# ScalarE sums for two group norms, a fifth weight tile, and the first pre-sum ahead of GpSimd's multiply

## The chip, the cores and the metric

The kernel runs on one core of a Trainium2 chip. A core has five engines that run side by side, each with its own queue of instructions in a fixed order: TensorE (PE, matmuls), VectorE (DVE), ScalarE (ACT), GpSimd (POOL) and SyncE (SP, which here only issues DMAs). They wait for one another by semaphores. The metric is device time in microseconds (us), here a median of three runs; one further execution was profiled.

## The reference

Two layers of "outlook attention" on an image batch x of shape (8, 56, 56, 384), float32. In each layer x is normalised by groups (32 groups of 12 channels, mean and variance over a whole image), and the layer's result is added to x:

```python
def _gn(v, G=32, eps=1e-5):
    g = v.reshape(B_, H_, W_, G, C_ // G)
    m = jnp.mean(g, axis=(1, 2, 4), keepdims=True)
    s = jnp.var(g, axis=(1, 2, 4), keepdims=True)
    return ((g - m) / jnp.sqrt(s + eps)).reshape(v.shape)
x = x + _L0_conv_ref(_gn(x), Wv, Wa, Wo)
x = x + _L1_conv_ref(_gn(x), W_attn, b_attn, W_v, b_v, W_proj, b_proj)
```

Layer 0 has 12 heads. For each pixel it projects x to values v and to 9 x 9 logits a head, takes a softmax over the last 9, weighs the 3 x 3 neighbourhood of v with each of the 9 rows, folds the 9 results back onto the 3 x 3 neighbourhood (a sum of overlapping patches), and projects with Wo. Layer 1 has 6 heads and one row of 9 weights a pixel.

What matters here: before a pixel of a layer can be normalised, the sums over its whole image must be known.

## The kernel before, in words

**Tiling.** The 8 images are worked on in 4 pairs (IMG = 2). A column x of both images, 112 rows, is the unit of layer 0: W = 56 columns a pair, 224 columns in all, one loop step each. Channels lie on the 128 partitions in 3 chunks (NCH). Columns go in groups of SB = 8: the 8 x 112 rows of a group fill 7 tiles of 128 (column j of the group, j = 0 to 6, brings 112 of its own rows and 16 rows of column 7). So a step with j = 7 (NTILE) has no projections of its own; its weights are gathered by DMAs in `share_out` (L664).

**A step of layer 0** (L942 to L985, `attend` L621). For each pi of 0 to 2 TensorE projects a third of the logits into a PSUM bank (288 columns, `project`), VectorE takes the maximum and subtracts it into the tile `at`, and `between(pi)` puts other work in that place of all queues. Then ScalarE takes exp of `at`, TensorE projects v, ScalarE copies v out, and `between(3)` follows. PE, DVE, ACT and POOL keep the order in which the program issues; nothing is reordered by a scheduler.

What `between` adds (L959 to L979), with the column that it works for:

- `normalise` (L694), for the column before: VectorE sums the exps (four adds, a reciprocal, a mask: "den"), GpSimd multiplies `at` with den (972 elements, the longest GpSimd operation).
- `presum` (L707), for two columns before: fold needs sums over neighbouring columns. GpSimd makes them in three operations into the tile `pre`; the first adds two terms of columns c and c - 1, the others need column c + 1, which is normalised in this step. In `between(3)` ScalarE copies two more terms into `pre`.
- `fold` (L741), for three columns before: ScalarE and VectorE write the weights `wts`; TensorE shifts rows with a 0/1 matrix into `pw` (four matmuls); two to four DMAs by SP bring the weights to a table in DRAM.
- `jobs` (L354, L809 `plan`): for each patch of PX = 7 columns, matmuls that contract values with weights (`pc`, read out to `yT` by ScalarE), and six `project_out` jobs (L851): three matmuls into `po`, VectorE adds the residual into `x1t`, and in the version before takes the batch statistics of layer 1's input (`bn_stats`, two images). Steps at which jobs are due are written out by hand in `plan`.
- `stats_chunk` (L461), for the next pair: VectorE transposes a third of a block of 4 columns of x (`xt`), takes the batch statistics of both images, and every third step SP stores the block in DRAM (`keep_block` L486). It runs in steps with c from 3 to 44 of pairs 0 to 2. Pair 0's own statistics are taken ahead of the loop, as there is no other work then.

`norm_params` (L272) turns the statistics into scale and bias: VectorE aggregates them, TensorE sums over the channels of a group with a matmul (`pgmean`, then `pgvar`), ScalarE takes a square root. It is in three parts, put into steps c = 45 to 47 (x, from `upkeep` L896) and, for layer 1's input, into the last job's step and the two after it (`norms`, L885 to L891).

**Buffers that the change touches.** `at` has 4 buffers (L630, L681): column c's is read until `presum(c + 1)` is through in step c + 3, so that step c + 4 takes the buffer in which c was. `pre` has 2, `x1t` 2, `xt` 2, PSUM 4 banks for projections, one each for `po`, `pw`.

**Layer 1** (L1022 onward) is a loop over the same columns with its own steps; the change adds a call there that does work in its first steps alone.

Of the kernel before, what the change touches and what calls it, by code (L numbers as in the profile page):

```python
# [15 lines left out]
def two_outlook_layers(  # L16
# [35 lines left out]
    P = 128  # L52
# [214 lines left out]
    def sort_columns(t, by, i, engine):  # L267
        engine(
            t[:, i].rearrange("k (j p) -> k j p", j=NCH), by[:, i].rearrange("k (p j) -> k j p", j=NCH)
        )  # L270

    def norm_params(st, name, params, key):  # L272

        mv = stat.tile([P, IMG, 2], F32, tag="mv", name=f"mv_{name}")

        def over_groups(src, what):
            pg = ps.tile([P, IMG], F32, tag="o", name=f"p{what}_{name}")
            matmul(pg, gmat, src, start=True, stop=True)
            g = stat.tile([P, IMG], F32, tag=what, name=f"{what}_{name}")
            vector.tensor_copy(g, pg)  # L280
            return g

        for b in range(IMG):
            vector.bn_aggr(mv[:, b, :], st[:, b].rearrange("p i n s -> p (i n) s"))
        yield
        mean = over_groups(mv[:, :, 0], "gmean")

        part = stat.tile([P, IMG], F32, tag="part", name=f"part_{name}")
        vector.tensor_sub(part, mv[:, :, 0], mean)
        vector.tensor_mul(part, part, part)  # L290
        vector.tensor_add(part, part, mv[:, :, 1])
        yield
        var = over_groups(part, "gvar")
        std = stat.tile([P, IMG], F32, tag="std", name=f"std_{name}")
        scalar.activation(std, var, AF.Sqrt, bias=eps_t)
        scale = const.tile([P, IMG], F32, name=f"scale_{name}")
# [86 lines left out]
    gpsimd.memset(zs[1][:, NZ0:], 0.0)  # L383
    zs = [z[:, :NZ0].rearrange("p (n e) -> p n e", n=NPY0) for z in zs]
    jobs, norms = Jobs(), Jobs()
    later = []

    def flush():
        while later:
# [32 lines left out]
    def layer0(late, pools):  # L422
# [38 lines left out]
        def stats_chunk(pair, blk, i):  # L461

            if blk == 0 and i == 0:
                stats[pair] = stat.tile([P, IMG, NCH, NBLK, 6], F32, tag="st0", name=f"st0_{pair}")
            if i == 0 and pair:
                xts[pair, blk] = block_tile(pair, blk)
            xr, xt = xrs[pair, blk], xts[pair, blk]
            if pair == 0:
                pt = bank(P, 0, XB * R).rearrange("p (m r) -> p m r", m=XB)
                for j in range(XB):  # L470
                    transpose(pt[:, j, :], xr[:, j, i::NCH], ident[:R, :R])
                scalar.copy(xt[:, :, i, :], pt)
            else:
                vector.transpose(
                    xt[:, :, i, :].rearrange("p m (k s) -> p s m k", s=NR), xr[:, :, :, i::NCH]
                )
            yield
            for b in range(IMG):
                vector.bn_stats(stats[pair][:, b, i, blk, :], xt[:, :, i, b * H : (b + 1) * H])
            if i == NCH - 1:  # L480
                del xrs[pair, blk]
                if pair:
                    keep_block(pair, blk)
            yield

        def keep_block(pair, blk):  # L486

# [133 lines left out]
        def attend(pair, c, between):  # L621

            nm = f"0_{pair}_{c}"
            k, j = divmod(c, SB)
            if j == NTILE:
                for n in range(K + 1):
                    between(n)
                return
            lhs = xns[(pair * W // SB + k) % 2][:, :, j, :]
            at = work.tile([P, K, K2, PH], F32, tag="at", name=f"at_{nm}", bufs=4)  # L630
            mx = work.tile([P, K, PH], F32, tag="mx", name=f"mx_{nm}", bufs=1)
            for pi in range(K):
# [31 lines left out]
        def share_out(pair, c):  # L664

            k, j = divmod(c, SB)
            at, last = attns[pair, c], lasts[(pair * W // SB + k) % 2]
            end = c - j + NTILE
            if j < NTILE - 2:
                later.append(  # L670
                    lambda: sync.dma_start(
                        bass.AP(
                            last.tensor, last.offset + j * PART * NA0,
                            [[H * NA0, IMG], [NA0, PART], [1, NA0]],
                        ),
                        at[R:].rearrange("p a b c -> p (a b c)"),
                    )
                )
                return
            if j == NTILE - 2:  # L680
                attns[pair, end] = work.tile([P, K, K2, PH], F32, tag="at", name=f"at_0_{pair}_{end}", bufs=4)  # L681
# [25 lines left out]
        def presum(pair, c):  # L707
# [17 lines left out]
                    gpsimd.tensor_tensor(dst, terms[0], terms[1], ALU.add)  # L725

            put(1, 2, of(0, 1, 2), of(-1, 1, 2))
            put(3, 1, of(0, 3, 1), of(1, 3, 1))
            put(2, 1, pre[:, :, 2:3, :], of(1, 2, 1)) if c + 1 < W else None
            pres[pair, c] = pre  # L730
# [78 lines left out]
        def plan(pair, px, first, second, last):  # L809
# [36 lines left out]
            if pair == NPAIR - 1 and px == NPX - 1:  # L846
                jobs.add(second[-1], clear_bands)
            if px == 0:
                st1s[pair] = stat.tile([P, IMG, NCH, 2 * NPX, 6], F32, tag="st1", name=f"st1_{pair}")

            def project_out(half, j):  # L851
                lo, hi = HALVES[half]
# [10 lines left out]
                for b in range(IMG):  # L863
                    vector.bn_stats(
                        st1s[pair][:, b, j, 2 * px + half, :],
                        x1t[:, j, : hi - lo, b * H : (b + 1) * H],
                    )
                if j == NCH - 1:
                    later.append(
                        lambda: sync.dma_start(  # L870
# [13 lines left out]
            if px == NPX - 1:  # L884
                def params_part(n):  # L885
                    if n == 0:
                        making["1"] = norm_params(st1s.pop(pair), f"1_{pair}", params1, pair)
                    next(making["1"])

                for n in range(3):  # L890
                    norms.add(last[-1] + n, lambda n=n: params_part(n))  # L891

        making = {}
        clearing = list(clears())
# [44 lines left out]
        for step in range(NPAIR * W + LAG):  # L939
# [4 lines left out]
            def weigh():  # L944

                normal = 1 <= step < NPAIR * W + 1 and (step - 1) % SB < NTILE
                if normal:
                    normalise(*divmod(step - 1, W))
                if normal and step % SB == NTILE:
                    share_out(*divmod(step - 1, W))  # L950
                if 2 <= step < NPAIR * W + 2:
                    summing.append(presum(*divmod(step - 2, W)))
                    next(summing[0])
                if normal and step % SB < NTILE:
                    share_out(*divmod(step - 1, W))
                if normal:
                    keep_v(*divmod(step - 1, W))

            def between(n):  # L959

                if n == 0:
                    next(turning, None)
                    weigh()
                    jobs.run(step, 1)
                elif n == 1:
                    if step % SB != NTILE:
                        next(folding, None)
                    next(turning, None)
                elif n == 2:
                    jobs.run(step, 1)  # L970
                    norms.run(step, 1)
                else:
                    for part in summing:
# [48 lines left out]
    def layer1(pools, base, last_of_layer0, late_w):  # L1022
# [226 lines left out]
        for step in range((NG + 1) * PX):  # L1249
# [23 lines left out]
            if g and m == moved:  # L1273
                move(done)
            jobs.run(base + step, 1)
            norms.run(base + step, 1)
            flush()
            store()
# [57 lines left out]
```

## Time and profile before

| what | value |
|---|---|
| median of 3 runs | 3263.03 us (3261.41 to 3264.24) |
| profiled execution | 3258.23 us |
| its span (first to last instruction) | 3256.5 us |
| granted TensorE clock, mean | 0.977 |
| VectorE batch statistics in the layer 0 loop | 636, of 0.33 to 0.39 us |
| ScalarE normalise, 128x672 / 128x504 | 0.95 / 0.81 us |
| ScalarE exp, 128x972 | 1.01 us, 196 of them |
| GpSimd multiply, 128x972 | 2.25 us |
| activation table loads | 17, of 1.28 us |

The profile's page has each engine's busy time; groups of instructions (line, engine, operation, output<-inputs, shapes, count, then busy time and mean ns of one); and waits (an engine's idle time in front of a group, by what ended it). Most instructions of the loop are issued through one helper and carry its line, L143 (L128 for matmuls), so groups are told apart by tile names. The windows view gives busy time by stretch of the span, with the granted clock (PEclk, 1.00 is full speed) and the DMA engines' share. Layer 0's loop runs from about 70 us to 2149 us.

### The profile page before, as it was taken

The page shows a single profiled execution, that of the slowest core. Times are in us where ns is not written, and L with a number is a line of the kernel's source. Part 1 is how long each engine was busy: PE and PEld are TensorE (multiplying, and loading weights), DVE is VectorE, ACT ScalarE, POOL GpSimd, SP SyncE. Part 2 cuts the span into 40 slices and gives each one's busy share as a digit, 9 for nine tenths or more (in the row PEclk, how much of TensorE's full clock was granted, in tenths as well). Part 3 has the DMA queues.
Part 4 walks back from the last instruction along what each step waited for, and adds up shares of the span by engine and source line. Part 5 has one row for each costly group of instructions (what it writes and reads, how often), then busy time and mean ns, then how long its engine had stood idle before and what let it go on. Part 6 is the DMA issues. An engine that isn't in the chain of part 4 may idle for free. (4 is left out here: it accounts for less than half of the span.)

```text
span 3256.5 us, 71940 instructions
## 1 busy us (share of the span) xinstructions
PE 3049.7 (94%) x27136; PEld 2044.7 (63%) x27136; DVE 2182.2 (67%) x5071; ACT 1020.7 (31%) x2736; POOL 1531.4 (47%) x2319
## 2 busy tenths in 40 slices
PE   6789999989999999999999999979999999999998
PEld 5556666666666766666666667745565656565655
DVE  5778777788887688887767677734555555555554
ACT  3233334333333433333334333322222222222221
POOL 2555445455445555454555555544434334343331
PEclk8999999999999999999999999989999999999999
DMA  9699997899998889998778788797888989989887
GB/s 285 193 280 307 294 283 244 275 297 285 280 281 292 271 265 288 302 305 269 259 252 297 258 286 284 228 336 211 224 237 229 247 222 243 237 235 232 242 227 170
DMA packets 745405, 850.80 MB, mean 261 GB/s; under 512 B 406286, under 2 KB 632210, under 8 KB 736738
## 3 DMA queue, kind: packets, MB, share of 16 engines
q1 hardware_dynamic: 647890, 711.32, 73.4%
q0 software_dynamic: 63824, 116.90, 11.4%
q10 hardware_dynamic: 33344, 17.98, 2.1%
q8 instruction: 214, 3.51, 0.5%
q14 instruction: 133, 1.09, 0.1%
HBM read 514.86 MB, written 322.17 MB: 257 GB/s over the span
## 5 line engine op out<-in xcount | busy, mean ns | idle before, releaser
L128 PE MATMUL bank<-wa_t,xn 128*128 128x288 f32 x3528 | 979.2, 416 | 3.3 <-ACT xn L143 3.3
L143 POOL TENSOR_TENSOR at<-at,den 128x972 f32<-128x972 f32 x196 | 440.6, 2248 | 898.2 <-DVE den L143 537.5
L128 PE MATMUL po<-yT,wo_t 128*128 128x448 f32 (+1 forms) x2304 | 822.5, 500 | 31.8 <-DVE x1t L143 25.7
L128 PEld LDWEIGHTS bank<-wa_t,xn 128*128 128x128 f32 x3528 | 659.0, 194 | 213.5 <-issue 21.2
L128 PEld LDWEIGHTS po<-yT,wo_t 128*128 128x128 f32 x2304 | 437.3, 192 | 348.9 <-issue 196.8
L143 ACT ACTIVATE at<-at 128x972 f32<-128x972 f32 (+1 forms) x228 | 215.2, 944 | 1090.1 <-DVE at L143 1075.9
L1111 POOL DMA_DIRECT2D at<-lgt x392 | 204.8, 526 | 594.3 <-DVE lgt L143 583.3
L128 PE MATMUL bank<-wc_t,xn 128*128 128x438 f32 x1176 | 477.5, 542 | 1.3 <-DMA wc_t<-in_wv 1.3
L143 ACT COPY yT<-pc 128x294 f32<-128x294 f32 (+2 forms) x512 | 193.1, 403 | 767.5 <-PE pc L128 767.0
L143 DVE TENSOR_REDUCE mx<-bank 128x36 f32<-128x324 f32 x588 | 284.3, 484 | 217.9 <-PE bank L128 211.8
L128 PEld LDWEIGHTS pc<-z,vp 121*32 121x32 f32 (+1 forms) x17664 | 342.5, 122 | 139.0 <-issue 84.3
L128 PE MATMUL bank<-wv_t,xn 128*128 128x384 f32 x1176 | 416.1, 491 | 0.0
L128 PE MATMUL pc<-z,vp 121*32 121x49 f32 (+1 forms) x17664 | 378.8, 220 | 33.6 <-ACT yT L143 19.4
L143 DVE TENSOR_TENSOR at<-bank,mx 128x324 f32<-128x324 f32 x588 | 291.5, 496 | 140.3 <-ACT pre L143 59.2
L128 PEld LDWEIGHTS bank<-wc_t,xn 128*128 128x128 f32 x1176 | 215.2, 190 | 176.0 <-issue 162.9
L128 PEld LDWEIGHTS bank<-wv_t,xn 128*128 128x128 f32 x1176 | 222.5, 191 | 133.1 <-issue 10.9
L143 POOL DMA_DIRECT2D vtab<-v x476 | 289.4, 612 | 15.9 <-DMA vtab<-zeros 4.6
L143 POOL TENSOR_TENSOR pre<-at,at 112x108 f32<-112x108 f32 (+1 forms) x440 | 224.2, 526 | 58.3 <-DMA at<-at 43.4
L143 DVE TENSOR_TENSOR lgt<-bank,ba_t 128x54 f32<-128x54 f32 x196 | 42.1, 215 | 305.0 <-PE bank L128 302.5
L128 PE MATMUL pw<-pre,shift 112*112 112x120 f32 x896 | 140.0, 280 | 86.4 <-POOL pre L143 31.5
L329 POOL DMA_DIRECT2D vtab<-v x392 | 211.6, 544 | 14.3 <-issue 7.4
L128 PEld LDWEIGHTS pw<-pre,shift 112*112 112x112 f32 x896 | 125.3, 184 | 133.5 <-issue 62.9
(110 smaller groups left out, 2724.8 us busy)
## 6 DMA issues: line engine op xcount, KB each, us to landing
z<-ztab SPq DMA_DIRECT2D x64, 2352.0 KB
vp<-vtab SPq DMA_DIRECT2D x64, 1536.0 KB
vp<-vtab SPq DMA_DIRECT2D x64, 945.0 KB
xres<-xT SPq DMA_DIRECT2D x32, 1176.0 KB
ztab<-wts SPq DMA_DIRECT2D x336, 110.2 KB
vtab<-v POOLq DMA_DIRECT2D x108, 336.0 KB, 6.5
xin<-xT SPq DMA_DIRECT2D x52, 672.0 KB
z<-ztab SPq DMA_DIRECT2D x128, 258.4 KB
```

What stands on the lines that cost most here:

```text
L128: tc.keep_in_program_order(nc.tensor.matmul(*args, **kwargs))
L143: return lambda *args, **kwargs: tc.keep_in_program_order(op(*args, **kwargs))
L329: queue.dma_start(bass.AP(table.tensor, table.offset + first, [*([line * step, count] for step, count in rows_of or ((1, rows),)), *([[(R ...
L1111: nc.gpsimd.dma_start(at_of(g_of)[row : row + n, m_of].rearrange("r k h -> r (k h)"), lg[lo : lo + n])
```

## The change

It does four things.

1. A class `Sums` keeps, per pair and layer, sums of (x - shift) and (x - shift) squared. ScalarE makes them as an additional output (`accum_out`) of an Identity and a Square activation over all 3 chunks of one image of a block; the ordinary output goes to a tile `unused` that nobody reads. `shift` is the mean of the first block, from six `bn_stats` and two `bn_aggr` on VectorE (`start`). x of pairs 1 to 3 and layer 1's input of all pairs are summed so; pair 0's x keeps the batch statistics. `sum_up` puts two activations (one image) into `between(1)` of the steps with c % 3 of 0 and 1 (both images at c = 45), `add_up` two into `between(2)`, one image a step. `norm_params` reads the sums by `mean_and_var`, for layer 1's input two steps later than before.
2. `at` has 5 buffers.
3. GpSimd's first operation of `presum` is issued ahead of `normalise`, the others where they were.
4. In `between(0)` VectorE's transpose of the next pair comes after `weigh` and the job, not before.

```diff
+        def start(self, parts):
+            st = stat.tile([P, IMG, NCH, 6], F32, tag="st_first", name=f"st_first_{self.name}", bufs=1)
+            mv = stat.tile([P, IMG, 2], F32, tag="mv_first", name=f"mv_first_{self.name}", bufs=1)
+            for b in range(IMG):
+                for i in range(NCH):
+                    vector.bn_stats(st[:, b, i], parts(b, i))
+                vector.bn_aggr(mv[:, b], st[:, b])
+            vector.tensor_scalar_mul(self.shift, mv[:, :, 0], -1.0)
+        def add(self, n, b, part):
...
+            for k, f in enumerate((AF.Identity, AF.Square)):
...
+                scalar.activation(
+                    to, part, f, bias=self.shift[:, b : b + 1], accum_out=self.sums[:, b, k, n : n + 1]
+                )
+        def mean_and_var(self, mv):
+            s = stat.tile([P, IMG, 2], F32, tag="s", name=f"s_{self.name}")
+            vector.tensor_reduce(s, self.sums, AX.X, ALU.add)
+            vector.tensor_scalar_mul(s, s, 1.0 / (NCH * W * H))
+            square = stat.tile([P, IMG], F32, tag="sq", name=f"sq_{self.name}")
+            vector.tensor_mul(square, s[:, :, 0], s[:, :, 0])
+            vector.tensor_sub(mv[:, :, 1], s[:, :, 1], square)
+            vector.tensor_sub(mv[:, :, 0], s[:, :, 0], self.shift)
...
+            if pair == 0:
+                for b in range(IMG):
+                    vector.bn_stats(stats[pair][:, b, i, blk, :], xt[:, :, i, b * H : (b + 1) * H])
...
+                    if blk == 0:
+                        stats[pair].start(lambda b, i: xt[:, :, i, b * H : (b + 1) * H])
+                    summed.append((stats[pair], blk, xt.rearrange("p m i r -> p i m r")))
...
-            at = work.tile([P, K, K2, PH], F32, tag="at", name=f"at_{nm}", bufs=4)
+            at = work.tile([P, K, K2, PH], F32, tag="at", name=f"at_{nm}", bufs=5)
...
             put(1, 2, of(0, 1, 2), of(-1, 1, 2))
+            yield
             put(3, 1, of(0, 3, 1), of(1, 3, 1))
...
-                for b in range(IMG):
-                    vector.bn_stats(
-                        st1s[pair][:, b, j, 2 * px + half, :],
-                        x1t[:, j, : hi - lo, b * H : (b + 1) * H],
-                    )
+                if j == NCH - 1:
+                    parts = x1t[:, :, : hi - lo]
+                    if not px and not half:
+                        st1s[pair].start(lambda b, i: parts[:, i, :, b * H : (b + 1) * H])
+                    for b in range(IMG):
+                        adding.append(
+                            lambda b=b: st1s[pair].add(2 * px + half, b, parts[:, :, :, b * H : (b + 1) * H])
+                        )
...
-                    norms.add(last[-1] + n, lambda n=n: params_part(n))
+                    norms.add(last[-1] + IMG + n, lambda n=n: params_part(n))
...
+                if 2 <= step < NPAIR * W + 2:
+                    summing.append(presum(*divmod(step - 2, W)))
+                    next(summing[0])
                 if normal:
                     normalise(*divmod(step - 1, W))
...
-                if 2 <= step < NPAIR * W + 2:
-                    summing.append(presum(*divmod(step - 2, W)))
-                    next(summing[0])
+                for part in summing:
+                    next(part)
...
                 if n == 0:
-                    next(turning, None)
                     weigh()
                     jobs.run(step, 1)
+                    next(turning, None)
                 elif n == 1:
...
                     next(turning, None)
+                    for b in range(IMG):
+                        if step % W == NBLK * NCH + 3 or (step % W) % NCH == b:
+                            sum_up(b)
                 elif n == 2:
                     jobs.run(step, 1)
+                    add_up()
                     norms.run(step, 1)
```

Layer 1's loop calls `add_up` once a step too, after its job.

More of the change, by code (lines that the diff above doesn't have):

```diff
@@ L270, in sort_columns, with __init__ @@
         )
+    class Sums:
+        def __init__(self, name, n):
+            self.name, self.n = name, n
+            self.sums = stat.tile([P, IMG, 2, n], F32, tag=f"sums{n}", name=f"sums_{name}")
+            self.shift = stat.tile([P, IMG], F32, tag=f"shift{n}", name=f"shift_{name}")
+        def start(self, parts):
[7 more added lines that the diff above has]
+        def add(self, n, b, part):
+            other = part.shape
+            for k, f in enumerate((AF.Identity, AF.Square)):
+                size = 1
+                for d in other[1:]:
+                    size *= d
+                to = stat.tile([P, 4 * NCH * H], F32, tag="unused", name=f"unused_{self.name}", bufs=1)
+                to = to[:, :size].rearrange("p (i m r) -> p i m r", i=other[1], m=other[2])
+                scalar.activation(
[9 more added lines that the diff above has]
+            vector.tensor_sub(mv[:, :, 0], s[:, :, 0], self.shift)
     def norm_params(st, name, params, key):
@@ L281, in over_groups @@
             return g
-        for b in range(IMG):
-            vector.bn_aggr(mv[:, b, :], st[:, b].rearrange("p i n s -> p (i n) s"))
+        if isinstance(st, Sums):
+            st.mean_and_var(mv)
+        else:
+            for b in range(IMG):
+                vector.bn_aggr(mv[:, b, :], st[:, b].rearrange("p i n s -> p (i n) s"))
         yield
@@ L385, in two_outlook_layers, with add_up @@
     jobs, norms = Jobs(), Jobs()
-    later = []
+    later, adding = [], []
+    def add_up():
+        if adding:
+            adding.pop(0)()
     def flush():
@@ L463, in stats_chunk @@
             if blk == 0 and i == 0:
-                stats[pair] = stat.tile([P, IMG, NCH, NBLK, 6], F32, tag="st0", name=f"st0_{pair}")
+                if pair:
+                    stats[pair] = Sums(f"0_{pair}", NBLK)
+                else:
+                    stats[pair] = stat.tile([P, IMG, NCH, NBLK, 6], F32, tag="st0", name=f"st0_{pair}", bufs=1)
             if i == 0 and pair:
@@ L477, in stats_chunk @@
             yield
-            for b in range(IMG):
-                vector.bn_stats(stats[pair][:, b, i, blk, :], xt[:, :, i, b * H : (b + 1) * H])
+            if pair == 0:
+                for b in range(IMG):
+                    vector.bn_stats(stats[pair][:, b, i, blk, :], xt[:, :, i, b * H : (b + 1) * H])
             if i == NCH - 1:
@@ L483, in stats_chunk, with sum_up @@
                     keep_block(pair, blk)
+                    if blk == 0:
+                        stats[pair].start(lambda b, i: xt[:, :, i, b * H : (b + 1) * H])
+                    summed.append((stats[pair], blk, xt.rearrange("p m i r -> p i m r")))
             yield
+        summed = []
+        def sum_up(b):
+            if summed:
+                sums, n, part = summed[0]
+                sums.add(n, b, part[:, :, :, b * H : (b + 1) * H])
+                if b == IMG - 1:
+                    summed.pop(0)
         def keep_block(pair, blk):
@@ L680, in share_out @@
             if j == NTILE - 2:
-                attns[pair, end] = work.tile([P, K, K2, PH], F32, tag="at", name=f"at_0_{pair}_{end}", bufs=4)
+                attns[pair, end] = work.tile([P, K, K2, PH], F32, tag="at", name=f"at_0_{pair}_{end}", bufs=5)
             whole = attns[pair, end]
@@ L848, in plan @@
             if px == 0:
-                st1s[pair] = stat.tile([P, IMG, NCH, 2 * NPX, 6], F32, tag="st1", name=f"st1_{pair}")
+                st1s[pair] = Sums(f"1_{pair}", 2 * NPX)
             def project_out(half, j):
@@ L862, in project_out @@
                 )
-                for b in range(IMG):
-                    vector.bn_stats(
-                        st1s[pair][:, b, j, 2 * px + half, :],
-                        x1t[:, j, : hi - lo, b * H : (b + 1) * H],
-                    )
+                if j == NCH - 1:
[6 more added lines that the diff above has]
+                        )
                 if j == NCH - 1:
@@ L968, in between @@
                     next(turning, None)
+                    for b in range(IMG):
+                        if step % W == NBLK * NCH + 3 or (step % W) % NCH == b:
+                            sum_up(b)
                 elif n == 2:
                     jobs.run(step, 1)
+                    add_up()
                     norms.run(step, 1)
@@ L1275, in layer1 @@
             jobs.run(base + step, 1)
+            add_up()
             norms.run(base + step, 1)
```

## The prediction

> **What bounds it now.** I read the page's first part, then busy time by stage, who TensorE waits for, then the timeline around one of those waits.
>
> ```profile
> PE 3049.7 (94%) x27136; PEld 2044.7 (63%) x27136; DVE 2182.2 (67%) x5071; ACT 1020.7 (31%) x2736; POOL 1531.4 (47%) x2319
> ```
>
> TensorE bounds the whole. Its matmuls are untouched, so a gain can only be idle TensorE time, or time at a lowered clock. Busy time by stage; the four are about layer 0's image pairs 0 to 3, and PEclk is the granted clock:
>
> ```profile
> core 0: us, PE busy (x) PEld busy (x) DVE busy (x) ACT busy (x) POOL busy (x), PEclk, DMA share, GB/s
> 70.00:590.00 520.00, 461.46 (x3914) 322.69 (x3913) 400.56 (x991) 176.61 (x464) 270.35 (x360) 0.96 0.86 266
> 590.00:1116.00 526.00, 494.29 (x4770) 345.65 (x4769) 417.27 (x1043) 185.07 (x489) 271.17 (x365) 0.98 0.90 282
> 1116.00:1642.00 526.00, 493.71 (x4773) 345.87 (x4773) 418.13 (x1045) 185.34 (x489) 271.92 (x367) 0.98 0.90 282
> 1642.00:2149.00 507.00, 482.58 (x4951) 342.08 (x4949) 351.35 (x909) 183.84 (x488) 274.64 (x376) 0.99 0.83 272
> ```
>
> Length less busy: TensorE idles 58.5, 31.7, 32.3 and 24.4 us, 147 in all. The lowered clock costs about (1 - clock) x length: 21, 11, 11 and 5, 48 in all. So layer 0 holds 195 us to win and no more. Pair 3 has no next pair to transpose and sum up: VectorE is 66 us less busy there, and the stage loses 29 us, not 43. That is the nearest row to this change.
>
> Who TensorE waits for (us, times, longest):
>
> ```profile
> PE pw L128 <- POOL pre L143: 31.5, 17, 5.9
> PE pw L128 <- issue: 31.4, 36, 3.1
> PE po L128 <- DVE x1t L143: 25.7, 18, 3.9
> PE pw L128 <- ACT pre L143: 23.5, 5, 8.3
> ...
> PE pc L128 <- ACT yT L143: 19.4, 10, 5.1
> PE pgmean L128 <- DVE mv L143: 10.8, 3, 4.5
> ```
>
> Most is `pw`, the shift matmul of fold, which needs ScalarE's copies into `pre`. One column of pair 1 in the timeline (start, length, idle before in brackets):
>
> ```profile
> 1005.17 0.69 DVE L143 BATCH_NORM_STATS2 st<-xt 128x6 f32<-128x224 f32 x2
> ...
> 1006.29 0.49 DVE L143 TENSOR_TENSOR at<-bank,mx 128x324 f32<-128x324 f32 x1
> ...
> 1006.82 1.01 ACT L143 ACTIVATE at<-at 128x972 f32<-128x972 f32 x1 [6.18 <-DVE at L143]
> ...
> 1008.46 0.50 DVE L143 TENSOR_TENSOR at<-bank,mx 128x324 f32<-128x324 f32 x1 [1.08 <-ACT pre L143]
> ...
> 1008.65 0.64 PE L128 MATMUL pw<-pre,shift 112*112 112x120 f32 x4 [0.87 <-issue]
> 1008.88 1.11 DVE L143 STREAM_TRANSPOSE xt<-xr 128x512 f32<-128x512 f32 x1
> ```
>
> This is a loop through VectorE: subtract, exp, copies into `pre`, and the next column's first subtract, which waits 1.08 us for those copies since they read the oldest of four `at` buffers. It comes round every 9.37 us (999.09 to 1008.46), while TensorE has 9.37 - 0.87 = 8.50 us of work. ScalarE sits idle 6.18 us before exp, 1043.6 / 196 = 5.3 us on average. Every eighth column (j = 7) has no projections; TensorE overtakes VectorE there and waits 1.4 to 5.1 us, and half the clock often follows.
>
> **The change part by part.** Durations are of the profiled execution: 3258.2 us, of which 3256.5 is span.
>
> *Off VectorE.* Of the 252 stats of x, 234 go (18 stay in `start`); of the 384 of layer 1's input, 360. By the busy times (83.2 us for 252, 66.0 + 54.8 for 384) that is 77 + 113 = 190 us. Per ordinary column with a transpose it takes 0.69 us out of the loop.
>
> *Onto ScalarE.* Blocks: 14 x 2 images x 2 functions x 3 pairs = 168 of 672 elements; layer 1's input: 14 x 2 x 2 x 4 = 224, half of 672 and half of 504. Rows: a normalise of 128x672 takes 0.95 us, of 128x504 0.81. The trace shows no accumulated output. Its read-out lies between 0 and 0.30 us (the 128x2 square root), a gain being excluded as work is added; I take the 128x1 activation, 0.20. So 280 x 1.15 + 112 x 1.01 = 435 us. A couple (Identity and Square) costs 2.3 us. Behind it in ScalarE's queue stand yT's copies, exp, v and `pre`'s copies; TensorE waits for yT and `pre`. Cover is the idle before exp: 5.4 to 8.5 us where a column has two couples (4.6 us), under 2 us in some five columns a pair. If it fails, exp is late by the excess. Two couples meet in 39 columns of pairs 0 to 2 (14, 14 and, as layer 1's sums begin late in pair 0, 11). I charge 1 us in eight columns of pairs 0 to 2, two thirds of it reaching TensorE: **-16**, bounds 0 and -45 (1.15 us for each of 39 two-couple columns).
>
> The Trainium skill, "ScalarE: Activation LUTs", section Rules for kernel authors, says to put add and mul on VectorE and not on ScalarE. In engine time the trace agrees: two activations (1.9 us) stand for three stats (3 x 0.37 = 1.1 us); by the rule the sum would be a loss of about 0.8 us a block and image. The rows decide otherwise, for VectorE closes the loop and ScalarE waits in it.
>
> *A fifth `at`.* The 1.08 us wait goes (VectorE waits 59.2 us for ScalarE's `pre`, 36.9 for GpSimd's), and GpSimd's 50.1 us in front of `at<-at`. Next late is VectorE's own work: 9.37 - 1.08 - 0.69 = 7.6 us, below TensorE's 8.5. So the `pw` gaps of 0.4 to 0.9 us close: 5.3 + 5.5 + 5.5 + 0.5 = 17 us over the pairs. Pair 0's first columns have no contractions and stay VectorE-bound; of their 20 us of gaps I take 9. **+26**, bounds 10 and 37.
>
> *The j = 7 columns* lose 32 + 19 + 20 + 15 = 87 us, TensorE's gaps there summed without pgmean. VectorE reaches the last subtract before them 0.69 + 1.08 = 1.8 us sooner, so each gap shrinks by up to that: 12 + 11.5 + 12 + 6 = **+41**, bounds 15 and 70. The den chain doesn't gain from the transposing moved behind it here: before, the transpose filled the wait for exp.
>
> *Statistics of a pair.* `mean_and_var` is five small VectorE operations (0.15 to 0.2 us each) and replaces two aggregations of 1.26 or 1.42 us. Two columns later, pgmean of layer 1's input leaves the short column 15, where TensorE waited 10.8 us for mv; some of it is the gap any j = 7 column has: **+7**, bounds 0 and 11. `start` adds seven bursts of six stats, two aggregations and a multiply, about 2.7 us each on VectorE; all sit 2 or more columns ahead of a j = 7, so I cost them at 0, bound -10.
>
> *GpSimd's first term* (0.64 us) runs in its wait for den (537.5 us over 96 waits); where GpSimd isn't idle it delays the multiply by as much. The other GpSimd operations and its DMA issues behind the multiply keep their order. ScalarE waits 100.2 us for the multiply, mostly at j = 7: taken as 0, bounds +-8. Transposes behind den make den 1.1 us earlier in ordinary columns, where GpSimd isn't late. No DMA is added; SP's block stores and loads stay where they are.
>
> *The clock.* It falls to half after the long gaps:
>
> ```profile
> 805.80:812.40 6.60, 4.96 (x58) 3.66 (x62) 5.25 (x14) 3.35 (x11) 4.71 (x6) 0.51 0.92 273
> ...
> 1710.00:1716.00 6.00, 4.06 (x17) 2.95 (x18) 3.17 (x9) 2.28 (x7) 4.37 (x8) 1.00 1.04 332
> ...
> 1918.40:1921.80 3.40, 2.89 (x100) 2.77 (x101) 1.16 (x4) 1.76 (x6) 3.38 (x5) 0.55 0.84 207
> ```
>
> The first follows a gap of 3.9 us. The second holds one of 2.6 and keeps the clock; the third holds one of 2.2 and loses it. With gaps near 2 us left, I take 20 of the 48 us back, bounds 5 and 40. "TensorE: Matmul & The Clock Gate", section Why this matters for your kernels, allows gaps up to about 3 us; by that rule nearly all 48 would return, 28 us more than I take. The 2.2 us gap speaks against it.
>
> **Sum:** 26 + 41 + 7 + 20 - 16 = 78 us. 3258.2 - 78 = 3180 for a run like the profiled one, which lies 4.8 us under the median of the runs shown (3263.0); against that median 3185. About 0.2% (7 us) is what a measurement of this kernel can tell from no change.
>
> **Rivals.**
> 1. *The gain stays small: 3240.* The j = 7 columns keep their lag, since den must wait for exp there anyhow and the transpose, once filler, now comes after it; the clock stays low. Then 26 less ScalarE's full 16, and about 13 of the 61 from j = 7 and clock: 23 us. For it: pair 3, with 66 us less on VectorE, won only about 14 us over pair 2. Against: the 1.08 us wait is of every pair. Chance 0.20, of 3222 to 3255.
> 2. *Nearly all bounds are met at the top: 3110.* Gaps and clock mostly go: 37 + 70 + 11 + 40 - 5 = 153. Chance 0.07.
> 3. *Slower: 3337.* Square shares no activation table with exp. The trace has 1283 ns a table load, around the square roots alone, and no Square. Then each of 196 couples brings two loads, 196 x 2 x 1.283 = 503 us on ScalarE, a couple costs 4.9 us, and the 39 columns with two couples need 9.7 us before exp against an idle of about 7.2, less the 1.8 that VectorE has come nearer: 4.3 us late each, 168 us, less the 94 of the gains: 74 lost. It decides from (5.4 + 94 / 39) / 2 = 3.9 us a couple. Chance 0.10. The skill, "ScalarE: Activation LUTs", section Table sets: the hidden batching unit, lists relu, copy, identity and abs in every set, and not square; by its 2.66 us a switch the loads would be 1043 us.
> 4. *No change.* Not doing what it says is hardly possible for the operations, but gains and ScalarE's delays can cancel within 7 us: 0.05.
>
> My forecast, 3135 to 3222, has 0.58. The range 3135 to 3250 adds nearly all of rival 1 and leaves out the rest. Faster 0.58 + 0.20 + 0.07 = 0.85, same 0.05, slower 0.10.
>
> **What would show it.** After: 42 batch statistics beside the first pair's 84; no wait of VectorE's `at` for `pre`; `pw` gaps under 1 us gone in columns 28 to 45; TensorE's idle in pairs 1 and 2 near 18 us each and clock 0.99; ScalarE near 1450 us busy, its idle before exp down to 2 to 4 us; table loads still 17. Wrong: more table loads; TensorE waiting more on yT or on ScalarE's `pre`; j = 7 gaps of 4 us as before.

## The result, and the profile after

The change made the kernel faster, by a quarter of what was predicted. The median went from 3263.64 us (3261.41 to 3265.27, 4 runs) to 3244.85 (3243.49 to 3246.89, 4 runs): a ratio of 0.9943, with a 95% interval of 0.9926 to 0.9961. That is 18.8 us where 78 were forecast. The time lies outside the forecast of 3135 to 3222 us; it lies inside the wider range to 3250 only because that takes in rival 1. The profiled executions differ by 11.3 us (3258.23 and 3246.89); the tallies below are of these.

The engines on the page after:

```profile
PE 3043.9 (94%) x27136; PEld 2041.3 (63%) x27136; DVE 2015.7 (62%) x4519; ACT 1386.3 (43%) x3584; POOL 1551.5 (48%) x2319
```

VectorE lost 552 instructions and 166 us. ScalarE got 848 instructions: 424 sums, and for each a second instruction that reads the accumulator out. Its groups show the prices (busy, mean ns, then idle time before them; the first block is of the kernel before, the second of after):

```profile
L143 ACT ACTIVATE at<-at 128x972 f32<-128x972 f32 (+1 forms) x228 | 215.2, 944 | 1090.1 <-DVE at L143 1075.9
```

```profile
L143 ACT ACTIVATE at<-at 128x972 f32<-128x972 f32 (+1 forms) x228 | 215.2, 944 | 475.2 <-DVE at L143 474.2 <-DMA at<-lgt 0.8
...
L143 ACT ACTIVATE unused<-xt,shift 128x672 f32<-128x672 f32 x168 | 142.8, 850 | 2.8
...
L143 ACT ACTIVATION_READ_ACCUMULATOR unused<-xt,shift 128x1 f32 x168 | 31.5, 188 | 0.0
```

ScalarE's idle time before exp fell from 1090 to 475 us. Table loads stayed at 17. Busy time by stage, layer 0's four pairs:

```profile
core 0: us, PE busy (x) PEld busy (x) DVE busy (x) ACT busy (x) POOL busy (x), PEclk, DMA share, GB/s
70.00:581.00 511.00, 460.28 (x3909) 323.64 (x3908) 362.31 (x855) 264.06 (x666) 275.28 (x361) 0.96 0.90 271
581.00:1107.00 526.00, 492.54 (x4769) 345.08 (x4768) 369.78 (x887) 289.52 (x729) 275.95 (x365) 0.98 0.92 282
1107.00:1628.00 521.00, 491.43 (x4768) 344.12 (x4767) 370.14 (x886) 289.52 (x729) 276.78 (x366) 0.98 0.94 284
1628.00:2130.00 502.00, 483.81 (x4954) 341.75 (x4952) 327.45 (x825) 238.26 (x621) 280.25 (x376) 0.99 0.84 274
```

Pairs 0 to 3 take 511, 526, 521 and 501 us, where they took 521, 526, 525 and 507: layer 0 won 19 us. The rest of the kernel lost 7.5 (1107.9 to 1115.4 us); there TensorE's `pc` waits 12.2 us for DMAs of `z`, where it waited 2.0 for these and 7.9 for a store. VectorE has 48 us less to do in pair 1, and the pair is as long as it was. What is late instead stands in the waits (us, times, longest), first before, then after:

```profile
DVE at L143 <- ACT pre L143: 59.2, 67, 1.1
...
ACT wts L143 <- DMA ztab<-wts: 44.1, 18, 8.8
...
DVE wts L143 <- DMA ztab<-wts: 16.9, 13, 10.7
...
POOL pre L143 <- DMA at<-last: 9.2, 2, 7.0
```

```profile
ACT at L143 <- DVE at L143: 474.2, 195, 11.5
...
ACT wts L143 <- DMA ztab<-wts: 189.4, 53, 14.5
...
POOL pre L143 <- DMA at<-last: 80.7, 11, 14.9
DVE wts L143 <- DMA ztab<-wts: 75.5, 30, 13.6
```

VectorE's wait of `at` for ScalarE's `pre` (59.2 us before) is gone. But ScalarE now stands 189.4 us before it may write `wts` (44.1 before), VectorE 75.5 (16.9 before): they wait for SP's earlier stores of the same buffer to land. There are four `wts` buffers, a column uses one or two of them, and one is written again two or three columns later. GpSimd's `pre` waits for the gather of column 7's weights (`at<-last`), 80.7 us against 9.2.

What one such wait does, in the timeline of pair 1 (start, length, what ran, idle before):

```profile
935.81 0.97 ACT L143 ACTIVATE wts<-pre,inside 112x36 f32<-112x36 f32 x4 [7.16 <-DMA ztab<-wts]
935.94 0.16 DVE L143 MEMSET wts<- 112x120 f32 x1 [4.07 <-PE pc L128]
...
936.66 0.84 ACT L143 ACTIVATE unused<-xt,shift 128x672 f32<-128x672 f32 x1
...
937.21 0.49 DVE L143 TENSOR_TENSOR at<-bank,mx 128x324 f32<-128x324 f32 x1
...
937.41 0.19 ACT L143 ACTIVATION_READ_ACCUMULATOR unused<-xt,shift 128x1 f32 x1
937.63 0.85 ACT L143 ACTIVATE unused<-xt,shift 128x672 f32<-128x672 f32 x1
...
938.48 1.00 ACT L143 ACTIVATE at<-at 128x972 f32<-128x972 f32 x1
...
939.74 0.46 ACT L143 COPY pre<-at 112x108 f32<-112x108 f32 x2
...
940.30 1.11 PE L128 MATMUL pw<-pre,shift 112*112 112x120 f32 x4 [2.82 <-issue]
```

ScalarE stands 7.16 us for a store. The sums come next in its queue, then exp, then the copies into `pre`; TensorE's `pw` stands 2.82 us and starts 0.1 us behind them. VectorE stands too: its own write of `wts` starts 0.13 us after ScalarE's (the profile puts that wait down to `pc`), and the subtract that exp needs, at 937.21, comes behind it. It ends at 937.70; the sums hold exp 0.8 us longer. Before, exp's operands came last, ScalarE had 5 us of idle time ahead of exp, and a late store was lost in that.

To see where the gain went I tallied, from each trace, TensorE's gaps over 0.15 us in layer 0's loop, apart for the place of the j = 7 columns (from exp of j = 6 to the next exp) and all other columns, and the time lost to the lowered clock, (1 - granted clock) x time. All in us; the names are those of the experiments:

| kernel | ratio to before | gaps at j = 7 | other gaps | lowered clock |
|---|---|---|---|---|
| before | 1 | 100.6 | 39.4 | 46.7 |
| after | 0.9943 | 67.3 | 61.3 | 42.0 |
| e1, after, six `wts` | 0.9854 | 66.0 | 43.2 | 41.8 |
| e3, after, no sums | 0.9891 | 72.4 | 45.6 | 39.3 |
| e4, after, less traffic | 0.9720 | 62.3 | 22.4 | 15.4 |
| e6, after, small transfers | 0.9741 | 62.6 | 23.1 | 18.8 |
| e12, after, six `wts`, small transfers | 0.9717 | 59.7 | 23.4 | 22.2 |
| e7, before, five `at` | 0.9924 | 90.8 | 31.9 | 47.0 |
| e8, before, sums | 0.9981 | 86.9 | 44.5 | 44.4 |
| e11, before, five `at`, six `wts` | 0.9916 | 100.1 | 29.5 | 50.8 |

The j = 7 gaps shrank by 33 us. The other gaps grew by 22: in pairs 1 and 2 from 6.9 and 6.7 to 18.1 and 15.1. The clock gave 5. That is 16 of layer 0's 19 us. Of the rest, 2 are an earlier start (the first exp at 69.6 us instead of 71.6); what remains lies outside these classes.

### The profile page after: what moved, and what is told of

Its sections match the earlier page's. It is cut to its first block, busy times and chain, and to the rows that moved or that the text cites. A ratio compares the mean times of both kernels' runs of the same rounds, so it can differ in the third digit from the quotient of the medians.

```text
span 3245.2 us, 72428 instructions
## 1 busy us (share of the span) xinstructions
PE 3043.9 (94%) x27136; PEld 2041.3 (63%) x27136; DVE 2015.7 (62%) x4519; ACT 1386.3 (43%) x3584; POOL 1551.5 (48%) x2319
## 5 line engine op out<-in xcount | busy, mean ns | idle before, releaser
L143 POOL TENSOR_TENSOR pre<-at,at 112x108 f32<-112x108 f32 (+1 forms) x440 | 239.4, 544 | 166.7 <-DMA at<-last 80.7
L143 ACT ACTIVATE unused<-x1t,shift 128x672 f32<-128x672 f32 (+1 forms) x256 | 200.7, 784 | 178.1 <-DVE x1t L143 152.9
L143 ACT ACTIVATE wts<-pre,inside 112x48 f32<-112x48 f32 (+4 forms) x672 | 179.7, 355 | 207.6 <-DMA ztab<-wts 189.4
```

The costliest lines, as they stand in the source:

```text
L143: return lambda *args, **kwargs: tc.keep_in_program_order(op(*args, **kwargs))
```

## The experiments

My theory: **the stores took VectorE's place.** With the fifth `at` ScalarE and VectorE reach `wts` sooner and meet stores not yet landed; the DMA engines are 0.92 to 0.94 busy in pairs 1 and 2. Rivals: ScalarE's sums themselves make exp late (the prediction's -16, larger than thought); the DMA engines carry too many bytes in general; SP's queue issues too many DMAs; the early first term or the later transposing costs what the others win. Where an expectation numbers its theories, 1 is the stores and 4 SP's queue. Every ratio is to the kernel before, run beside it.

**e1: six buffers for `wts`, in after.** A buffer then comes back after three or four columns, so each store has more time. For the room, `unused` becomes bfloat16 and takes the statistics' place, and layer 1's two bias rows are loaded only when layer 1 starts.

```diff
-        NWT = 4
+        NWT = 6
-            n = (0, 1, 2, 3, 0, 1, 3, 2, 3, 0, 1)[sx]
+            n = (4, 5, 2, 4, 0, 1, 2, 3, 0, 1, 3)[sx]
```

> The kernel after, with six buffers of wts in place of four, in an order in which a buffer comes back after three or four columns and not after two. (Room for them: the unread output lies as bf16 on pair 0's statistics, and layer 1's two bias rows are loaded in layer 1.) Theory 1, late stores: the loop that VectorE left ran into the wait for the stores of wts, which land late because the DMA engines are 90 to 94% busy in layer 0. Then ScalarE's wait for ztab<-wts falls from 189 us to under 50, VectorE's from 76 to under 20, and the time from 3245 to about 3200. Theory 2, ScalarE's queue: the 768 added ScalarE instructions themselves make yT and pre late. Then the waits on the stores fall too, but the time stays within 8 us of 3245.

Measured: 3220.49 us, 0.9854 (0.9839 to 0.9870). Beside after's 0.9943 that is 29 us, intervals apart, though short of the 3200 that was expected. ScalarE's wait for stores fell from 189.4 to 4.1 us, VectorE's to 2.5, and pair 1 from 526 to 513 us. TensorE's other gaps went back to 43.2 only, and the clock not at all. GpSimd waits longer for the gather:

```profile
POOL pre L144 <- DMA at<-last: 112.4, 13, 14.5
...
ACT wts L144 <- DMA ztab<-wts: 4.1, 5, 1.5
```

Not all of the 29 us are the buffers'. In the five kernels that load the bias rows late (e1, e2, e7, e11, e12) layer 0's first exp starts at 63.8 to 66.4 us, in the nine others at 69.1 to 72.0: some 5 us of their gains are this earlier start. From the first exp to the last, e1 takes 24.6 us less than after. So the stores cost about 25 us.

**e2: the same six buffers in before.** The edit is that of e1, without `unused`.

> The kernel before, with the same six buffers of wts. Theory 1: before, the stores were a small part (44 us of ScalarE's waits, 17 of VectorE's), since VectorE closed the loop: 3264 goes to 3255 to 3262. Theory 2: no change, 3264 within 4 us.

Measured: 3259.02 us, 0.9974 (0.9962 to 0.9986), 8 us, most of which the earlier start can explain (first exp at 63.8 us instead of 71.6). Before, these buffers were hardly in the way: TensorE's gaps are as before (98.0 and 41.7).

**e3: no sums, in after.** `start`, `mean_and_var` and all else stay; the activations of `add` go.

```diff
+            gpsimd.memset(self.sums, 1.0)
...
-                scalar.activation(
-                    to, part, f, bias=self.shift[:, b : b + 1], accum_out=self.sums[:, b, k, n : n + 1]
-                )
```

> The kernel after without the accumulating activations; it leaves out the sums, which are a constant instead. Theory 1: ScalarE is 370 us less busy, but the stores of wts land as late as before; its wait for them stays over 120 us and the time is 3225 to 3245. Theory 2: the time falls to 3170 to 3195, what the prediction's other terms give (94 us under 3264).

Measured: 3231.90 us, 0.9891 (0.9876 to 0.9907): 17 us better than after. ScalarE's wait for stores is not smaller but larger:

```profile
ACT wts L143 <- DMA ztab<-wts: 217.9, 57, 14.2
```

So the sums don't cause the wait; they lengthen what stands behind it in the queue, and the other gaps fall from 61.3 to 45.6 without them.

**e4 and e5: less traffic, in after and in before.** Of the next pair's x only the first two blocks are loaded, and the residual is loaded once instead of per patch. The compute engines' instructions stay.

```diff
+            if pair or px:
+                xres[pair, px] = kept_res[0]
+                return
...
-                    stats_load(pair + 1, blk + 1, sync, xr_tile(pair + 1, blk + 1))
+                    if blk == 0:
+                        stats_load(pair + 1, blk + 1, sync, xr_tile(pair + 1, blk + 1))
+                    else:
+                        xrs[pair + 1, blk + 1] = xr_tile(pair + 1, blk + 1)
```

> The kernel after with about a tenth of layer 0's DMA traffic left out: of the next pair's x only the first two blocks are loaded (the later ones are summed from old data), and the residual is loaded once and not for every patch. Theory 1: the stores land sooner, ScalarE's wait for ztab<-wts falls under 100 us, the time to 3205 to 3225. Theory 2: DMA busy falls, the time stays within 8 us of 3245.

> The kernel before with the same tenth of layer 0's DMA traffic left out (next pair's x loaded for two blocks alone, the residual loaded once). Theory 1, the bound moved: before, VectorE's loop closed each step, so less traffic helps it little: 3264 goes to 3245 to 3262, against 73 us for the kernel after. Theory 3, traffic bounds both alike and the change had nothing to win: before gains as much as after did, 60 to 80 us, to about 3195.

Measured: after 3176.92 us, 0.9720 (0.9706 to 0.9733), before 3254.18 us, 0.9969 (0.9959 to 0.9979). The same cut is worth 73 us to after and 10 to before; for after 20 to 40 were expected. Pairs 1 and 2 of e4:

```profile
561.00:1060.00 499.00, 483.03 (x4771) 341.34 (x4770) 370.31 (x887) 290.59 (x729) 276.43 (x366) 1.00 0.83 260
1060.00:1559.00 499.00, 482.61 (x4772) 340.73 (x4771) 371.55 (x889) 290.91 (x731) 276.96 (x367) 1.00 0.83 260
```

and of e5:

```profile
588.00:1114.00 526.00, 493.56 (x4772) 345.11 (x4771) 417.71 (x1044) 185.28 (x488) 271.85 (x367) 0.98 0.80 247
1114.00:1640.00 526.00, 493.38 (x4769) 344.51 (x4768) 416.80 (x1042) 184.95 (x488) 271.01 (x365) 0.97 0.80 246
```

With fewer bytes the changed kernel's pairs take 499 us at full clock and TensorE idles 16 in each: what the prediction described (18 us, clock 0.99). The kernel before takes its 526 us at a DMA share of 0.80 as at 0.90. It was held by VectorE's loop; after is held by the transfers. In e5 the gaps stay at 97.3 (j = 7) and 39.1 us. ScalarE's wait for stores in e4:

```profile
ACT wts L143 <- DMA ztab<-wts: 31.2, 13, 9.3
```

**e6: as many DMAs, each smaller, in after.** It tells the size of the traffic from the number of issues: the later blocks of x are loaded at a quarter, the residuals at a seventh of their size.

```diff
+                if blk > 1:
+                    queue.dma_start(
+                        xr[b * Q : b * Q + LANES, :, 0, :], by_quadrant(x, pair * R, blk * XB, 1, b)
+                    )
+                    continue
...
+            if pair or px:
+                xres[pair, px] = kept_res[0]
+                later.append(
+                    lambda: sync.dma_start(kept_res[0][:, :1], xTs[pair][:, px * PX : px * PX + 1])
+                )
+                return
```

> The kernel after with the same loads cut in size and not in number: the later blocks of the next pair's x are loaded at a quarter of their size, the residuals after the first at a seventh; what isn't loaded is old data. SyncE issues as many DMAs as in the kernel after. Theory 1, the bytes on the DMA engines: most of the 73 us that leaving the loads out gave stays, 45 to 65 us, time 3185 to 3205. Theory 4, SyncE's queue (an issue that stands behind slow issues): hardly anything stays, 3235 to 3250.

Measured: 3178.98 us, 0.9741 (0.9726 to 0.9755), beside e4's 0.9720 (0.9706 to 0.9733). Nearly all of e4's gain is there with every issue in place, so the number of issues isn't what makes the stores late; the amount of traffic is (over the whole kernel bytes and packets both fell by some 6%, and the two weren't told apart).

SP's queue is not cleared by this, for its issues themselves last longer in after. In pairs 1 and 2 they take 536 us in before, 698 in after and 551 in e6. The larger store of `wts` is issued a median of 0.97 us behind VectorE's last write of `wts` in after (a tenth over 6.8), where it is 0.03 in before and in e6 (a tenth over 3.1 and 3.3). Part of the stores' lateness thus arises before they are issued.

**e7: the fifth `at` alone, in before.** For the room, one buffer for x's statistics, and the bias rows as in e1.

```diff
-            at = work.tile([P, K, K2, PH], F32, tag="at", name=f"at_{nm}", bufs=4)
+            at = work.tile([P, K, K2, PH], F32, tag="at", name=f"at_{nm}", bufs=5)
```

> The kernel before with the fifth weight tile alone (room for it: one buffer of pair 0's statistics, layer 1's two bias rows loaded in layer 1). By the prediction's loop the 1.08 us wait goes and VectorE's own 8.3 us a column stand against TensorE's 8.5: a gain of 15 to 30 us, 3235 to 3250. If the stores of wts close the loop at once, or VectorE's own work does, under 8 us: 3256 to 3264.

Measured: 3239.01 us, 0.9924 (0.9912 to 0.9937). The fifth tile alone gives 25 us, some 5 of them by the earlier start; that is as much as the whole change. The waits for transfers come with it, without any sum on ScalarE:

```profile
ACT wts L143 <- DMA ztab<-wts: 132.1, 44, 13.1
...
POOL pre L143 <- DMA at<-last: 70.8, 11, 13.7
```

**e8: the change with four `at`,** and with both moves of the order undone.

```diff
-            at = work.tile([P, K, K2, PH], F32, tag="at", name=f"at_{nm}", bufs=5)
+            at = work.tile([P, K, K2, PH], F32, tag="at", name=f"at_{nm}", bufs=4)
```

> The kernel before with the ScalarE sums alone (four weight tiles, the transpose first, the first pre-sum behind the multiply). VectorE loses 0.69 us a column, ScalarE gains its 370 us. Theory 1: a gain of 5 to 20 us, 3244 to 3259, with the 1.08 us waits of the first subtract still there. Theory 2, ScalarE's queue: no gain or a loss, 3262 to 3285.

Measured: 3258.84 us, 0.9981 (0.9968 to 0.9993): 6 us. VectorE still waits 55.9 us for `pre`. ScalarE waits 146.7 us for stores, against 44.1 before, so the sums lengthen this wait without the fifth tile too; what it costs here isn't shown.

**e9 and e10: one move undone each, in after.** e9 puts the transpose ahead of `weigh` and the job again, e10 issues the first term behind `normalise` again.

```diff
                 if n == 0:
+                    next(turning, None)
                     weigh()
                     jobs.run(step, 1)
-                    next(turning, None)
```

```diff
-                if 2 <= step < NPAIR * W + 2:
-                    summing.append(presum(*divmod(step - 2, W)))
-                    next(summing[0])
                 if normal:
                     normalise(*divmod(step - 1, W))
...
+                if 2 <= step < NPAIR * W + 2:
+                    summing.append(presum(*divmod(step - 2, W)))
+                    next(summing[0])
```

> The kernel after with VectorE's transpose back in front of den and the job (before's place). The prediction costed the move at nothing. If den's place matters (GpSimd's multiply 1.1 us later in ordinary columns, nothing in j = 7 columns, where the transpose fills the wait for exp): 5 to 15 us slower than after in ordinary columns, or the same faster by the j = 7 columns. Theory 1 (stores bound): within 5 us of after, ratio 0.993 to 0.996.

> The kernel after with GpSimd's first pre-sum back behind the multiply. The prediction costed it at 0, bounds 8 us either way. Theory 1: pre comes 0.64 us later where GpSimd waited for den, ScalarE's wts and the stores with it, so up to 8 us slower, ratio 0.994 to 0.9965. If the early term holds up the multiply more than it helps: faster than after, 0.991 to 0.994.

Measured: e9 3250.48 us, 0.9958 (0.9945 to 0.9970); e10 3243.17 us, 0.9937 (0.9922 to 0.9951). Neither interval is apart from after's 0.9926 to 0.9961. The early first term is worth nothing that can be measured; the later transpose perhaps 5 us, which stays inconclusive.

**e11: five `at` and six `wts` in before,** without the sums and the moves: the edits of e7 and e2 together, with one buffer for each of the two statistics.

> The kernel before with five weight tiles and six buffers of wts, without the ScalarE sums and the two moves. Against six wts with the whole change (ratio 0.9854) it gives what the sums and the moves are worth once the stores are no wait. Prediction's loop: VectorE 8.3 us a column with its statistics, just under TensorE's 8.5, and 0.69 us more lag in each j = 7 column: 5 to 15 us slower than 0.9854, 0.987 to 0.990. If the sums are worth nothing: 0.9854 within 0.0015.

Measured: 3237.02 us, 0.9916 (0.9902 to 0.9929). Without the sums, free stores add nothing to the fifth tile (0.9924), though ScalarE waits 132.1 us for stores in e7 and 3.9 here. With the sums (e1 against after) they add some 25 us. So in e1 the sums and the moves are worth some 20 us over e11, more than the 5 to 15 that were expected, and the gaps at j = 7 show where: 100.1 in e11, 66.0 in e1.

**e12: six `wts` and small transfers in after:** the edits of e1 and e6 together.

> The kernel after with six buffers of wts and with the smaller loads of x and residuals. If the bytes only bind through the stores of wts, either cure alone is enough and both give what smaller loads gave, ratio 0.973 to 0.975. If bytes also bind elsewhere (gathers of the j = 7 column, z tables), six wts add 5 to 20 us: 0.968 to 0.972.

Measured: 3173.26 us, 0.9717 (0.9703 to 0.9730), beside e6's 0.9741 (0.9726 to 0.9755); the intervals touch, and the earlier start lies in the difference: from the first exp to the last the two take 1970.0 and 1967.4 us. With small transfers four buffers are enough. With full ones, six buffers still leave 45 us (0.9854 against 0.9717) to transfers other than these stores. The gather's wait is a candidate, as it falls from e1's 112.4 us to 9.8, and so are the loads of `z`; neither was tried alone, and how the 45 us divide stays open.

e1 is the fastest of the kernels that do all of the work: 0.9854 of before.

## Why the prediction was wrong, step by step

*What bounds it now* was right, and e5 shows it: a DMA share of 0.80 instead of 0.90 brings before only 10 us. The fifth tile opens the loop through VectorE, and alone it gives some 20 us (e7, without the earlier start), beside the +26 taken.

*"Next late is VectorE's own work: 9.37 - 1.08 - 0.69 = 7.6 us, below TensorE's 8.5."* This step failed. VectorE's work was indeed short enough, as e4 shows, but it wasn't next. The stores of `wts` (about 25 us, e1) and other transfers (45 us more, e12) were, at a DMA share of 0.92 to 0.94. The waits of before had them: 44.1 us of ScalarE's idle time and 16.9 of VectorE's were put down to `ztab<-wts`, and the share was 0.90. I named the engines in the loop and no transfer; "no DMA is added; SP's block stores and loads stay where they are" was true and beside the point, for a transfer needn't move to become late: the engine that waits for it can arrive sooner, and it can land later. The stores did land later (a median of 5.5 to 6.0 us from their issue, 3.9 in before; see the last section) and some were issued later. How much each of the three adds to the wait, and why the load rose with the same bytes, isn't shown. One of the prediction's own signs of being wrong came with it: TensorE's waits for `yT` in layer 0 rose from 17.0 to 30.5 us, and are 9.4 in e1. The terms then went so:

- *Ordinary columns, +26:* the small `pw` gaps of columns 28 to 45 closed as said. But gaps of 2.8 to 4.7 us opened in columns 16, 24, 37 and 45 of pair 1, and the tally is -22; TensorE idles 33 and 30 us in pairs 1 and 2, not 18. With less traffic it is +17 (e4), near the predicted 17 without pair 0's 9.
- *j = 7 columns and pgmean, +41 and +7:* 33 together, the one large term that mostly came in; e4 has 38. The mechanism holds for the two parts of the 1.8 us together only: with the fifth tile and no sums the gaps are 90.8 (e7) and 100.1 (e11), with sums and four tiles 86.9 (e8).
- *The clock, +20:* 5, as long gaps stayed as many. In after's pair 1 each of the five gaps of 2.8 to 4.7 us brought 3.4 us of lowered clock, and of the nine of 1.1 to 1.9 us one did. In e4, where the term is 31, pairs 1 and 2 have four gaps of 2.1 to 2.7 us, and one of them (2.3) brought it. In pairs 1 and 2 of all 14 traces lowered clock set in during the gap or within 2 us after it for none of the 88 gaps of 0.9 to 1.5 us, 19 of 95 up to 2, 25 of 49 up to 3, 12 of 16 up to 3.5, and all 46 longer ones. The Trainium skill, "TensorE: Matmul & The Clock Gate", section Why this matters for your kernels, advises against gaps of over about 3 us; here shorter ones cost clock too, so neither its 3 us nor my one gap of 2.2 us is a sharp bound.
- *ScalarE, -16:* e3 makes it 17 in time. The size is right, the place is not: with the sums in place and less traffic (e4) the gaps outside j = 7 are 0.9 us in each of pairs 1 and 2, so it is paid behind a late store, not by couples that outlast exp's slack. The estimated 435 us are 423 by the groups: 256 sums of layer 1's input where I had counted 224 (16 halves of patches, not 14), 128x672 at 0.85 us instead of 0.95, and a read-out of 0.19, near the 0.20 taken. The page's busy time rose by 366, in part because a read-out begins before its activation ends (937.41 against 937.50 in the timeline).
- *GpSimd's first term, 0; `start`, 0:* nothing measurable (e10); `start` was not tried alone.
- *Behind layer 0:* -7.5 us, for which the prediction had no term. That part is 1111 to 1116 us long in the faster variants, against 1107.9; no experiment was made on its cause.

*The rivals.* The time is that of rival 1 (3240), but not by its mechanism: it let the j = 7 columns keep their lag, and those are what improved. Rival 3 fell: Square brings no table load. Rival 2 wasn't met even where transfers were cut: e4 wins 91 us of its 153, and 62.3 us of gaps at j = 7 stay. None of the rivals was a transfer, and that is the gap in the list.

*Adds on ScalarE.* The prediction set aside what the Trainium skill, "ScalarE: Activation LUTs", section Rules for kernel authors, says of adds and multiplies. The runs bear that out only where the stores are out of the way: beside the fifth tile the sums and moves bring nothing with four `wts` (after's 0.9943, e7's 0.9924 with its earlier start, intervals overlapping) and some 20 us with six (e1, e11).

## What to carry to other kernels

When a change takes away the wait that closes a loop, cost every other wait in the loop again with the loop shortened, transfers too: here a small wait for a DMA at a busy share of 0.9 was the next bound, and writing its buffer again a column or two later removed it. Two limits in series hide each other: sums alone (0.9981), six buffers alone (0.9974) and less traffic alone (0.9969) each looked nearly worthless, and together with the fifth tile they are the larger part of the gain. The length of a wait isn't its price: 132 us of ScalarE's waits for stores in e7 cost nothing that can be measured, as e11 shows. An extra operation in an idle engine cost little here until something ahead of it in the same queue was late. And an experiment's side edit, such as the bias rows loaded late, needs its own price.

## What the hardware showed

- An accumulating activation is followed by an instruction of its own on ScalarE, which takes 0.19 us; the activation of 128x672 took 0.85 us.
- Stores landed later at a higher load. From issue to the last packet, the larger stores of `wts` in pairs 1 and 2 of after took a median of 5.5 to 6.0 us (a tenth over 11.4, at most 15.8) at a DMA share of 0.92 to 0.94, and in e4 3.4 to 3.5 us (a tenth over 8.6, at most 13.0) at 0.83. The other kernels lie along this: 2.4 to 2.5 us in e5 at 0.80, 4.1 to 4.3 in e6 at 0.87, 3.9 in before at 0.90, 5.1 to 5.3 in e7 at 0.94.
- SP's issue of these stores took longer too: 0.70 us on average in before's pairs 1 and 2, 1.02 in after's, 0.80 in e6's.
